# Layer 1's mixer: fewer, wider small products, B and C convolved as one block, and the slice bias as a float32r product

## The chip, the core and the metric

One Trainium2 chip, one of its cores. The metric is the device time in microseconds (us) of one execution of the whole program, as the median of several executions. A profiled execution gives the trace from which durations are read; it has a time of its own.

## The reference

Two layers on x (32 samples of 512 tokens by 256 features) with an integer adjacency matrix for each sample. Each layer is a graph stage and a feed-forward stage, each behind a layer norm and added to x. The change touches the second layer's feed-forward stage alone:

```python
fx = (x @ W_fx.T + b_fx).reshape(B, N, H, P).transpose(0, 2, 1, 3)
xm = (x @ W_x.T + b_x).reshape(B, N, H, P).transpose(0, 2, 1, 3)
sw = softmax((xm @ W_slice.T + b_slice) / temp, axis=-1)        # 8 heads, 64 slices
snorm = sw.sum(2)
st = einsum('bhnc,bhng->bhgc', fx, sw) / (snorm + 1e-05)[..., None]
ot = _hydra(st.transpose(0, 2, 1, 3).reshape(B, G, 512), ...)   # 64 slice tokens of 512
out = einsum('bhgc,bhng->bhnc', ot (by heads), sw)
return out.transpose(0, 2, 1, 3).reshape(B, N, 512) @ out_w.T + out_b

def _hydra(u, ...):                                  # a scan in both directions over 64 tokens
    zxbcdt = u @ in_w.T                              # z 512, x 512, B 64, C 64, dt 2 * 8
    dt = softplus(dt + dt_bias)                      # the second eight with the tokens reversed
    x, B, C = silu(causal convolution of width 3 over x, B and C)
    h = h * exp(-dt * exp(A_log)) + dt * B * x;  y = h . C        # each token, each head
    y = y_forward + y_backward + x * (x @ fcD.T + D)
    yg = y * silu(z)
    return (yg * rsqrt(mean(yg ** 2) + 1e-05) * norm_w) @ out_w.T
```

## The kernel before

Layer 0 takes the first 2400 us or so; near its end layer 1's constants are loaded and transposed a piece at a time between its steps (`load_T`). Layer 1 then goes through the samples with two generators. `attentions` prepares and computes the graph stage sample by sample. `mixer(g)` is the feed-forward stage of a pair of samples, g = 0 to 15. The mixer is the driver: each of its `yield n` gives credit by which the attention of later samples is advanced, so that both are woven into one program. From that the framework fixes the order of instructions on each engine, by its own estimate of when operands are ready; on the chip each engine goes through its list in order and waits on semaphores. PSUM banks of the mixer and most of the attention come from one pool ("any", four banks); work tiles of 128x512 of the mixer come from one rotating tag ("inner", six).

A round of the mixer, for samples 2g and 2g+1, in the order of the program:

- `slices` for each sample: layer norm (L1131, L1133), transposes (x4T, L1142); then for each of four token tiles the slice logits `lgp` (L1335, two float32 products of 512 columns), exp on ScalarE into `sw` (L1336), and on VectorE the product with `ebsl`, the exponential of the slice bias spread over all partitions (L1337), the sum over 64 slices of each head (L1340), its reciprocal (L1341) and the product with it (L1342). Then `yTp` (L1347) sums the tokens by slice weight, `swp` (L1352) transposes sw, and its copy on ScalarE gives the slice sums `rn` (L1353), of which VectorE takes the reciprocal (L1355).
- `tokens`: `uTp` (L1366) applies W_fx for each head. `rnp` (L1372) spreads the reciprocals over the partitions of their head: 16 products of 64x64, the weights being one column of rn repeated. `scale` (L1375) copies that out of PSUM, and VectorE makes `uT` (L1379, L1381): channels on partitions, 2 x 64 tokens in columns.
- `scan`, projection: `xp` (L1400, 16 products with 128 columns) gives x, `bcp` (L1409) B and C on 64 partitions each, in two column blocks; `dtp` (L1428) the step sizes in 16 products of 64x8 (forward and reversed halves put where they are needed) and 4 more of 128x16 (L1393); `zp` (L1393) z in 4 products of 512 columns. ScalarE copies x and B, C into padded tiles (`xpad` L1404, `bpad` L1413); VectorE convolves (`conv`, L1417 and L1419); ScalarE applies silu (L1455 for x, L1462 for B and C, L1450 for z) and, for the softplus, exp (L1437) and Ln (L1443), each change of function with a table load.
- `scan`, the rest: `gp` (L1487) is C times B, `segp` (L1491) the sums of log decays, from `seg` (L1481); `xtp`, `qp` (L1496, L1501); VectorE builds `mix` (L1505 to L1510); `yp` (L1517) is 16 products of 64x64, sample by sample, head by head; y (L1520 to L1522) is transposed (`yTp`, L1527), multiplied by the output weights (`oTp`, L1535); four products `msp` (L1543) put the mean squares on the partitions where `rms` (L1546, a power on GpSimd at L1547) is needed; `vp` (L1557) applies out_w, 64x64 weights and 256 columns, alternating between the two halves of the array.
- `unslice` for each sample: `outp` (L1567) and the sum into x (L1569), then the store.

In the attention, `att` (L1213) makes the weights on VectorE from `own`, a row that goes through DRAM and comes back spread over the partitions (L1200); `avp` and `adp` (L1249, L1254) multiply; `norm` (L1290 to L1304) is its layer norm on VectorE, with a power on GpSimd (L1300) in its middle; GpSimd also adds beta, the attention's bias and outb (L1167, L1189, L1328) and gathers x rows (L1154).

On PE a float32 product shows as two rows in the trace, each of which streams all columns; L434's product in layer 0, with both operands float32r, shows as one.

Of the kernel before, what the change touches and what calls it, by code (L numbers as in the profile page):

```python
# [8 lines left out]
F32 = mybir.dt.float32  # L9
# [855 lines left out]
def layer1_plain(tc, ident, eps, x2s, ranks, adj, w, out, over, ps):  # L865
# [35 lines left out]
    with ExitStack() as ctx:  # L901
# [14 lines left out]
        ones = ctile("ones", [P, P])  # L916
# [36 lines left out]
        bc_w = const("bc_w", [S, 2, KW], w["hy_conv_w"][DI:].rearrange("(c p) k -> p c k", p=S))  # L953
        bc_b = const("bc_b", [S, 2], w["hy_conv_b"][DI:].rearrange("(c p) -> p c", p=S))
        skip = const("skip", [P, H], w["hy_D"].partition_broadcast(P))
        dtb = ctile("dtb", [P, 4, H])
        for i in range(4):
            nc.sync.dma_start(dtb[:, i, :], w["hy_dt_bias"].partition_broadcast(P))
# [21 lines left out]

        wfxT = ctile("wfxT", [P, DC, DI])
        wsl = ctile("wsl", [P, DC, H, G])
        ebsl = ctile("ebsl", [P, H * G])
# [6 lines left out]
        with tc.tile_pool(name="raw", bufs=2, side="right") as raw:  # L990
# [16 lines left out]
            yield from load_T(inT, w["hy_in_w"], "in")  # L1007
# [48 lines left out]
            nc.sync.dma_start(ebsl, bsl_row.partition_broadcast(P))  # L1056
# [7 lines left out]
            nc.vector.tensor_reduce(most[:, 1:2], ebsl, AX.X, ALU.max)  # L1064
            nc.vector.tensor_reduce(most[:, 2:3], ebsl, AX.X, ALU.min)
            for i, limit, op in ((0, SMALL_S, ALU.is_gt), (1, SMALL_B, ALU.is_gt), (2, -SMALL_B, ALU.is_lt)):
                nc.vector.tensor_scalar(over[:, 2 * AH + i : 2 * AH + i + 1], most[:, i : i + 1], limit, None, op)
            nc.scalar.activation(ebsl, ebsl, AF.Exp)
# [249 lines left out]
        def slices(b, j, yT, rn):  # L1318
# [13 lines left out]
            for t in range(NT):  # L1332
                pf = psum("any", f"lgp{b}_{t}")
                for c in range(DC):
                    nc.tensor.matmul(pf, xnT[:, c, t * P : (t + 1) * P], wsl[:, c, :], start=c == 0, stop=c == DC - 1)  # L1335
                nc.scalar.activation(sw[:, t, :], pf, AF.Exp)  # L1336
                nc.vector.tensor_mul(sw[:, t, :], sw[:, t, :], ebsl)  # L1337
# [45 lines left out]
        def scan(g, uT):  # L1383
# [14 lines left out]
            for k in range(KC):  # L1398
                for c in range(KC):
                    nc.tensor.matmul(px[:, k * T : (k + 1) * T], inT[:, c, DI + k * P : DI + (k + 1) * P],  # L1400
                                     uT[:, c, :], start=c == 0, stop=c == KC - 1)
# [838 lines left out]
```

## Time and profile before

| What | us |
|---|---|
| median of 3 runs | 4462.75 (4462.54 to 4462.93) |
| profiled execution, its own time | 4459.08 |
| its span, first to last instruction | 4456.4 |
| PE busy | 3922.0 (88%) |
| VectorE (DVE) busy | 3347.2 (75%) |
| ScalarE (ACT) busy | 2291.6 (51%) |
| GpSimd (POOL) busy | 1718.8 (39%) |

Mean granted TensorE clock: 0.948. The rounds of the mixer can be told by `xp`, which starts at 2534.0, 2661.9, 2784.6 and so on to 4164.1, 4284.7 and 4390.4 us: 14 rounds of 125 us on average, and a last one with no attention beside it. In the tables of the profile, a group's line has engine, operation, output and inputs, shape, count; behind the first bar the busy time in us and the mean duration of one in ns; behind the second the engine's idle time just before these instructions and what ended it. A mean duration on PE holds the pipeline's depth, so the rate of products is read from the distance of their starts. The chain of work that ended last is followed back from the last instruction, at each step to what released it.

### The profile page before, as it was taken

The numbers are of one execution on the slowest core, as the hardware profiler recorded it, in microseconds if no ns is written. First come the engines' busy times: TensorE is split into PE (matmuls) and PEld (weight loads), VectorE is DVE, ScalarE is ACT, GpSimd is POOL, SyncE is SP. The second block draws the span as 40 slices with busy tenths as digits, with TensorE's granted clock in tenths as the row PEclk, the third lists the DMA queues.
The fourth block names the chain that finished last, engine by engine and source line by source line (L and its number), as shares of the span: only waits on it lengthen the run. The fifth ranks groups of instructions, "written<-read, shape, count | busy, mean of one in ns | idle before, by whom it ended". The sixth has DMA issues, their size and how long they took to land.

```text
span 4456.4 us, 57911 instructions
## 1 busy us (share of the span) xinstructions
PE 3922.0 (88%) x20311; PEld 2470.6 (55%) x20311; DVE 3347.2 (75%) x7008; ACT 2291.6 (51%) x4756; POOL 1718.8 (39%) x2036
## 2 busy tenths in 40 slices
PE   5568898899988999888997899999999999999987
PEld 4454565566656656545554455555555555555555
DVE  6668887897788987877766777767677877778763
ACT  3345565566564665556654544544545444454433
POOL 2357644664446644454314232332222232332220
PEclk8679999999999999989998999999999999999998
DMA  5546543664436543564422111111111111111100
GB/s 133 160 144 223 190 130 122 210 200 139 156 117 213 187 147 129 162 201 167 138 81 67 36 53 57 56 48 58 51 43 42 53 55 55 58 48 58 41 15 16
DMA packets 235107, 474.21 MB, mean 106 GB/s; under 512 B 38299, under 2 KB 114075, under 8 KB 234804
## 3 DMA queue, kind: packets, MB, share of 16 engines
q0 software_dynamic: 98688, 315.94, 22.2%
q1 hardware_dynamic: 136116, 154.46, 11.0%
q8 instruction: 162, 2.65, 0.2%
q14 instruction: 141, 1.16, 0.1%
HBM read 413.16 MB, written 57.16 MB: 106 GB/s over the span
## 4 chain that ended last, share of the span: by engine, by line
DVE 34%; PE 32%; DMA 11%; issue 9%; POOL 9%; ACT 5%; SPq 0%; POOLq 0%; DVEq 0%; ACTq 0%
DVE att L1213 5%; DVE acc L637 4%; PE clsp L623 3%; PE avp L1249 3%; PE po L652 3%; PE gatep L623 3%; DMA rows<-table,xs 2%; PE yTp L1347 2%; DVE sw L1337 2%; DVE sw L1342 2%; DVE best L598 2%; DMA rows<-table,tops 2%; DVE sst L1340 2%; DMA best<-table,xs 2%; PE xp L1400 1%
## 5 line engine op out<-in xcount | busy, mean ns | idle before, releaser
L623 PE MATMUL clsp<-xnT,wc 128*128 128x512 f32 x1024 | 520.8, 627 | 49.7 <-ACT cls L625 37.6
L623 PE MATMUL gatep<-xnT,wg 128*128 128x512 f32 x1024 | 499.8, 607 | 10.5 <-ACT gate L625 7.7
L652 PE MATMUL po<-wd,acc 128*128 128x256 f32 x2048 | 455.4, 381 | 6.1 <-DVE acc L641 3.8
L1213 DVE SCALAR_TENSOR_TENSOR att<-own,other,mask 128x512 f32<-128x512 f32 x512 | 392.9, 796 | 79.0 <-DMA own<-ownd 79.0
L652 PEld LDWEIGHTS po<-wd,acc 128*128 128x128 f32 x2048 | 388.3, 191 | 72.1 <-issue 9.2
L598 DVE SCALAR_TENSOR_TENSOR best<-rows,xs,best 128x1024 f32<-128x1024 f32 x212 | 274.4, 1295 | 121.9 <-ACT best L592 76.4
L637 DVE SCALAR_TENSOR_TENSOR acc<-past,fld,acc 128x512 f32<-128x512 f32 x448 | 345.7, 775 | 24.9 <-ACT past L636 16.9
L632 ACT ACTIVATE acc<-tz,fld 128x512 f32<-128x512 f32 x256 | 198.8, 777 | 269.3 <-PE tz L630 240.1
L623 PEld LDWEIGHTS gatep<-xnT,wg 128*128 128x128 f32 x1024 | 196.0, 196 | 252.3 <-issue 197.9
L636 ACT ACTIVATE past<-tz,fld 128x512 f32<-128x512 f32 x448 | 291.4, 693 | 68.1 <-DVE acc L637 66.6
L1347 PE MATMUL yTp<-sw,x 128*128 128x512 f32 x512 | 264.6, 655 | 64.3 <-DVE sw L1342 59.6
L595 POOL DMA_INDIRECT rows<-table,xs x212 | 249.5, 1177 | 171.6 <-DVE best L598 119.0
L1249 PE MATMUL avp<-att,hv 128*32 128x512 f32 x2048 | 298.9, 607 | 5.6 <-DVE att L1213 5.6
L623 PEld LDWEIGHTS clsp<-xnT,wc 128*128 128x128 f32 x1024 | 181.5, 198 | 188.1 <-issue 111.8
L434 PE MATMUL pm<-h,adj 128*128 128x258 f32 (+1 forms) x1024 | 181.2, 324 | 99.9 <-DVE keep L427 33.7
L1300 POOL TENSOR_TENSOR mu<-mu,eps 128x16 f32<-128x16 f32 x32 | 111.6, 3487 | 391.1 <-DVE mu L1299 391.0
L1335 PE MATMUL lgp<-wsl,x4T 128*128 128x512 f32 x512 | 242.8, 613 | 15.7 <-ACT sw L1336 6.8
L1154 POOL DMA_INDIRECT x<-x2s,ranks x128 | 135.9, 1062 | 298.1 <-DVE att L1213 148.1
L625 ACT ACTIVATE gate<-gatep,fld 128x512 f32<-128x512 f32 x256 | 175.5, 685 | 142.6 <-PE gatep L623 123.8
L553 POOL DMA_INDIRECT xs<-rows_of,order x128 | 156.1, 1219 | 221.5 <-DVE acc L637 100.8
L1567 PE MATMUL outp<-v,swT 128*128 128x256 f32 x1024 | 227.6, 381 | 0.0
L625 ACT ACTIVATE cls<-clsp,fld 128x512 f32<-128x512 f32 x256 | 176.1, 688 | 93.9 <-PE clsp L623 55.6
(599 smaller groups left out, 8978.1 us busy)
## 6 DMA issues: line engine op xcount, KB each, us to landing
adj<-in_adj POOLq DMA_DIRECT2D x128, 256.0 KB
ai<-in_adj SPq DMA_DIRECT2D x128, 256.0 KB
own<-ownd SPq DMA_DIRECT2D x128, 256.0 KB
rows_of<-keep SPq DMA_DIRECT2D x32, 550.0 KB
x<-in_x SPq DMA_DIRECT2D x32, 512.0 KB
x2s<-xs SPq DMA_DIRECT2D x32, 512.0 KB
out<-x SPq DMA_DIRECT2D x32, 512.0 KB
rows<-table,xs POOLq DMA_INDIRECT x212
```

The costliest lines, as they stand in the source:

```text
L595: nc.gpsimd.indirect_dma_start(out=row, out_offset=None, in_=table, in_offset=bass.IndirectOffsetOnAxis(ap=idxs[:, k : k + 1].bitcast(U32) ...
L598: nc.vector.scalar_tensor_tensor(m, row, vals[:, k : k + 1], m, ALU.add, ALU.max)
L623: nc.tensor.matmul(pf, wf[:, c, f * P : (f + 1) * P], xnT[:, c, :], start=c == 0, stop=c == DC - 1)
L625: nc.scalar.activation(o, pf, fn, bias=fld[:, f, bf : bf + 1], scale=1.0 if fn == AF.Gelu else 0.5)
L636: nc.scalar.activation(r, z, AF.Relu, bias=fld[:, f, AT + b : AT + b + 1])
L637: nc.vector.scalar_tensor_tensor(y, r, fld[:, f, CH + b : CH + b + 1], y, ALU.mult, ALU.add)
L652: nc.tensor.matmul(po[:, i, :], acc[f][:, t * P : (t + 1) * P], wd[:, f, :], start=f == 0, stop=f == FC - 1)
L1213: nc.vector.scalar_tensor_tensor(e, own[h], other[:, j, h : h + 1], mask[:, j, :], ALU.max, ALU.mult)
L1249: nc.tensor.matmul(pv[p][k * HW : (k + 1) * HW, :], hv[:, j, h, e : e + HW], weighed[b, h, j], **ends)
L1335: nc.tensor.matmul(pf, xnT[:, c, t * P : (t + 1) * P], wsl[:, c, :], start=c == 0, stop=c == DC - 1)
L1347: nc.tensor.matmul(py, xn[:, t, c * P : (c + 1) * P], sw[:, t, :], start=t == 0, stop=t == NT - 1)
L1567: nc.tensor.matmul(po[:, :D], swT[:, k, t * P : (t + 1) * P], v[:, k, :], start=k == 0, stop=k == KC - 1)
```

## The change

- Slice bias: the logits' bank starts with a product of two partitions by 512 columns, both operands float32r (a row of ones as weights, `brow` as the moving operand: the bias rounded to float32r and, on the second partition, what the rounding left), and the product with `ebsl` on VectorE is gone. `ebsl` is not made; `brow` is.
- Slice norms: VectorE makes `spread`, the reciprocals times an identity, 128x512, and one product with `same` (ones in the two diagonal blocks of 64) takes the place of the 16 of `rnp`.
- Projection: the columns of `inT` are put in the order dt, z, x, B, C. B and C come from one set of 4 products with 128 outputs, on 128 partitions; dt and the first half of z from 4 products of 272 columns into the same bank, the second half of z from 4 of 256. The reversed halves of dt are put in place by four small VectorE sums instead of products. `bc_w`, `bc_b`, `bpad` and `bcT` are 128 partitions high, and B and C's convolution is written ahead of x's.
- `gp` and `yp` loop over samples inside and heads (or directions) outside.
- `msp` is gone: four small VectorE operations write `rms` across partitions.

The diff, without the constants' shapes:

```diff
+        same = ctile("same", [P, P])
+        nc.gpsimd.memset(same, 0.0)
+        ident2 = ctile("ident2", [P, C])
+        for i in range(P // C):
+            half = slice(i * C, (i + 1) * C)
+            nc.gpsimd.memset(same[half, half], 1.0)
+            nc.gpsimd.tensor_copy(ident2[half], ident[half, half])
...
-        ebsl = ctile("ebsl", [P, H * G])
+        brow = cst.tile([2, H * G], F32R, tag="brow", name="brow")
...
-            yield from load_T(inT, w["hy_in_w"], "in")
+            yield from load_T(inT[:, :, 2 * H :], w["hy_in_w"][:DT0], "in")
+            yield from load_T(inT[:, :, : 2 * H], w["hy_in_w"][DT0:], "dt")
...
-            nc.sync.dma_start(ebsl, bsl_row.partition_broadcast(P))
+            both, least = (raw.tile([P, DI], F32, tag=f"raw{DI}", name=f"bias{i}")[:2] for i in range(2))
+            nc.sync.dma_start(both, bsl_row.partition_broadcast(2))
+            nc.scalar.copy(brow, both)
+            nc.vector.tensor_sub(least, both, brow.bitcast(F32))
+            nc.vector.tensor_scalar(least, least, ident[:2, 1:2], None, ALU.mult)
+            nc.vector.scalar_tensor_tensor(brow, brow.bitcast(F32), ident[:2, 0:1], least, ALU.mult, ALU.add)
...
-            nc.scalar.activation(ebsl, ebsl, AF.Exp)
...
                 pf = psum("any", f"lgp{b}_{t}")
+                nc.tensor.matmul(pf, short_ones[:2], brow, start=True, stop=False)
                 for c in range(DC):
-                    nc.tensor.matmul(pf, xnT[:, c, t * P : (t + 1) * P], wsl[:, c, :], start=c == 0, stop=c == DC - 1)
+                    nc.tensor.matmul(pf, xnT[:, c, t * P : (t + 1) * P], wsl[:, c, :], start=False, stop=c == DC - 1)
                 nc.scalar.activation(sw[:, t, :], pf, AF.Exp)
-                nc.vector.tensor_mul(sw[:, t, :], sw[:, t, :], ebsl)
                 s = sw[:, t, :].rearrange("p (h g) -> p h g", h=H)
...
         def tokens(g, yT, rn, uT):
+            spread = inner(f"spread{g}").rearrange("p (k j g) -> p k j g", k=KC, j=GB)
+            four = [P, KC, GB, G]
+            nc.vector.tensor_tensor(spread, rn.rearrange("p j k -> p k j").unsqueeze(3).to_broadcast(four),
+                                    ident2.unsqueeze(1).unsqueeze(1).to_broadcast(four), ALU.mult)
 
             pu, pn = psum("any", f"uTp{g}"), psum("any", f"rnp{g}")
-            uv, nv = (p.rearrange("p (k j g) -> p k j g", k=KC, j=GB) for p in (pu, pn))
+            uv = pu.rearrange("p (k j g) -> p k j g", k=KC, j=GB)
             for k in range(KC):
                 for i in range(P // C):
                     half, h = slice(i * C, (i + 1) * C), k * (P // C) + i
                     for c in range(DC):
                         nc.tensor.matmul(uv[half, k], wfxT[:, c, h * C : (h + 1) * C], yT[:, c, h],
                                          start=c == 0, stop=c == DC - 1)
-            for k in range(KC):
-                for i in range(P // C):
-                    half = slice(i * C, (i + 1) * C)
-                    for j in range(GB):
-                        nc.tensor.matmul(nv[half, k, j, :], rn[:, j, k : k + 1].to_broadcast([P, C]), ident[:, half],
-                                         start=True, stop=True)
+            nc.tensor.matmul(pn, same, spread.rearrange("p k j g -> p (k j g)"), start=True, stop=True)
             scale = inner(f"scale{g}")
...
                 for c in range(KC):
-                    nc.tensor.matmul(px[:, k * T : (k + 1) * T], inT[:, c, DI + k * P : DI + (k + 1) * P],
-                                     uT[:, c, :], start=c == 0, stop=c == KC - 1)
+                    x0 = 2 * H + DI + k * P
+                    nc.tensor.matmul(px[:, k * T : (k + 1) * T], inT[:, c, x0 : x0 + P], uT[:, c, :],
+                                     start=c == 0, stop=c == KC - 1)
             xpad = sb.tile([P, KC, GB, LP], F32, tag="xpad", name=f"xpad{g}", bufs=1)
             nc.gpsimd.memset(xpad[:, :, :, : KW - 1], 0.0)
             nc.scalar.copy(xpad[:, :, :, KW - 1 :], px.rearrange("p (k j l) -> p k j l", k=KC, j=GB))
-            pb = psum("any", f"bcp{g}")
-            for i in range(2):
-                c0 = 2 * DI + i * S
-                for c in range(KC):
-                    nc.tensor.matmul(pb[:S, i * T : (i + 1) * T], inT[:, c, c0 : c0 + S], uT[:, c, :],
-                                     start=c == 0, stop=c == KC - 1)
-            bpad = sb.tile([S, 2, GB, LP], F32, tag="bpad", name=f"bpad{g}", bufs=1)
-            nc.gpsimd.memset(bpad[:, :, :, : KW - 1], 0.0)
-            nc.scalar.copy(bpad[:, :, :, KW - 1 :],
-                           pb[:S, : 2 * T].rearrange("p (k j l) -> p k j l", k=2, j=GB))
+            pb, pz = psum("any", f"bcp{g}"), psum("any", f"zp{g}")
+            for c in range(KC):
+                nc.tensor.matmul(pb[:, :T], inT[:, c, DIN - P :], uT[:, c, :], start=c == 0, stop=c == KC - 1)
+            first = 2 * H + DI // 2
+            tok_matmul(pb[:, T : T + first], 0, first)
+            tok_matmul(pz[:, : DI // 2], first, DI // 2)
+            bpad = sb.tile([P, GB, LP], F32, tag="bpad", name=f"bpad{g}", bufs=1)
+            nc.gpsimd.memset(bpad[:, :, : KW - 1], 0.0)
+            nc.scalar.copy(bpad[:, :, KW - 1 :], pb[:, :T].rearrange("p (j l) -> p j l", j=GB))
...
 
-            pd = psum("any", f"dtp{g}")
-            for j in range(GB):
-                for i in range(2):
-                    for c in range(KC):
-                        nc.tensor.matmul(pd[i * G : (i + 1) * G, j * H : (j + 1) * H],
-                                         uT[:, c, j * G : (j + 1) * G],
-                                         inT[:, c, DT0 + i * H : DT0 + (i + 1) * H],
-                                         start=c == 0, stop=c == KC - 1)
-            tok_matmul(pd[:, 2 * H : 4 * H], DT0, 2 * H)
+            pd = pb[:, T : T + 2 * H]
             sp = sb.tile([P, 5, 4 * H], F32, tag="sp", name=f"sp{g}")
             v, e, u, r, dt = (sp[:, i, :] for i in range(5))
-            nc.vector.tensor_add(v, pd[:, : 4 * H], dtb.rearrange("p i h -> p (i h)"))
+            nc.vector.tensor_add(v[:, 2 * H :], pd, dtb.rearrange("p i h -> p (i h)"))
+            for i in range(2):
+                for j in range(GB):
+                    half = slice(j * G, (j + 1) * G)
+                    nc.vector.tensor_add(v[i * G : (i + 1) * G, j * H : (j + 1) * H],
+                                         pd[half, i * H : (i + 1) * H], dtb[half, 0, :])
             nc.vector.scalar_tensor_tensor(e, v, -1.0, v, ALU.mult, ALU.min)
...
 
-            pz = psum("any", f"zp{g}")
-            tok_matmul(pz, 0, DI)
             z = sb.tile([P, DI], F32, tag="z", name=f"z{g}", bufs=1)
-            nc.scalar.activation(z, pz, AF.Silu)
+            nc.scalar.activation(z[:, : DI // 2], pb[:, T + 2 * H : T + first], AF.Silu)
+            nc.scalar.activation(z[:, DI // 2 :], pz[:, : DI // 2], AF.Silu)
+            bcT = sb.tile([P, GB, G], F32, tag="bcT", name=f"bcT{g}", bufs=1)
+            cpad = sb.tile([S, GB, G + 2], F32, tag="cpad", name=f"cpad{g}", bufs=1)
+            nc.gpsimd.memset(cpad[:, :, 0 : G + 2 : G + 1], 0.0)
+            conv(bpad, bc_w, bcT)
+            for half, dst in ((slice(0, S), bcT[:S]), (slice(S, P), cpad[:, :, 1 : G + 1])):
+                nc.scalar.activation(dst, bcT[half], AF.Silu, bias=bc_b[half])
             xT = inner(f"xT{g}")
             for k in range(KC):
                 dst = chunks(xT)[:, k, :]
                 conv(xpad[:, k], conv_w[:, k, :], dst.rearrange("p (j l) -> p j l", j=GB))
                 nc.scalar.activation(dst, dst, AF.Silu, bias=conv_b[:, k : k + 1])
-            bcT = sb.tile([S, 2, GB, G], F32, tag="bcT", name=f"bcT{g}", bufs=1)
-            cpad = sb.tile([S, GB, G + 2], F32, tag="cpad", name=f"cpad{g}", bufs=1)
-            nc.gpsimd.memset(cpad[:, :, 0 : G + 2 : G + 1], 0.0)
-            for i in range(2):
-                conv(bpad[:, i], bc_w[:, i, :], bcT[:, i])
-                dst = bcT[:, 0] if i == 0 else cpad[:, :, 1 : G + 1]
-                nc.scalar.activation(dst, bcT[:, i], AF.Silu, bias=bc_b[:, i : i + 1])
-
-
...
             pg = psum("any", f"gp{g}")
-            for j in range(GB):
-                for i in range(2):
-                    nc.tensor.matmul(pg[j * G : (j + 1) * G, i * G : (i + 1) * G], bcT[:, 0, j, :],
+            for i in range(2):
+                for j in range(GB):
+                    nc.tensor.matmul(pg[j * G : (j + 1) * G, i * G : (i + 1) * G], bcT[:S, j, :],
                                      cpad[:, j, 2 * i : 2 * i + G], start=True, stop=True)
...
             py = psum("any", f"yp{g}")
-            for j in range(GB):
-                half = slice(j * G, (j + 1) * G)
-                for h in range(H):
+            for h in range(H):
+                for j in range(GB):
+                    half = slice(j * G, (j + 1) * G)
                     nc.tensor.matmul(py[half, h * C : (h + 1) * C], heads(mix)[half, h, :],
...
 
-            pm = psum("any", f"msp{g}")
+            rms = sb.tile([P, GB], F32, tag="rms", name=f"rms{g}")
             for j in range(GB):
                 for i in range(P // C):
-                    nc.tensor.matmul(pm[i * G : (i + 1) * G, j : j + 1], ident[:, j * G : (j + 1) * G], ms,
-                                     start=True, stop=True)
-            rms = sb.tile([P, GB], F32, tag="rms", name=f"rms{g}")
-            nc.vector.tensor_scalar(rms, pm[:, :GB], 1.0 / DI, LN_EPS, ALU.mult, ALU.add)
+                    nc.vector.tensor_scalar(rms[i * G : (i + 1) * G, j : j + 1], ms[j * G : (j + 1) * G], 1.0 / DI, LN_EPS,
+                                            ALU.mult, ALU.add)
             nc.gpsimd.tensor_tensor(rms, rms, eps[:, 1:2].to_broadcast([P, GB]), ALU.pow)
```

More of the change, by code (lines that the diff above doesn't have):

```diff
@@ L914, in psum @@
             return ps.tile([P, N], F32, tag=tag, name=name)
-        ones = ctile("ones", [P, P])
+        short_ones = cst.tile([P, P], F32R, tag="ones", name="ones")
+        ones = short_ones.bitcast(F32)
         nc.gpsimd.memset(ones, 1.0)
@@ L952, in layer1_plain @@
         conv_b = const("conv_b", [P, KC], w["hy_conv_b"][:DI].rearrange("(c p) -> p c", p=P))
-        bc_w = const("bc_w", [S, 2, KW], w["hy_conv_w"][DI:].rearrange("(c p) k -> p c k", p=S))
-        bc_b = const("bc_b", [S, 2], w["hy_conv_b"][DI:].rearrange("(c p) -> p c", p=S))
+        bc_w = const("bc_w", [P, KW], w["hy_conv_w"][DI:])
+        bc_b = const("bc_b", [P, 1], w["hy_conv_b"][DI:].rearrange("(p o) -> p o", o=1))
         skip = const("skip", [P, H], w["hy_D"].partition_broadcast(P))
-        dtb = ctile("dtb", [P, 4, H])
-        for i in range(4):
+        dtb = ctile("dtb", [P, 2, H])
+        for i in range(2):
             nc.sync.dma_start(dtb[:, i, :], w["hy_dt_bias"].partition_broadcast(P))
@@ L1063, in layer1_plain @@
             nc.vector.tensor_reduce(most[:, 0:1], pn, AX.X, ALU.max)
[L1064 to L1065 removed]
+            nc.gpsimd.memset(most[:, 1:], 0.0)
+            nc.vector.tensor_reduce(most[:2, 1:2], both, AX.X, ALU.max)
+            nc.vector.tensor_reduce(most[:2, 2:3], both, AX.X, ALU.min)
             for i, limit, op in ((0, SMALL_S, ALU.is_gt), (1, SMALL_B, ALU.is_gt), (2, -SMALL_B, ALU.is_lt)):
                 nc.vector.tensor_scalar(over[:, 2 * AH + i : 2 * AH + i + 1], most[:, i : i + 1], limit, None, op)
[L1068 removed]
         se = ctx.enter_context(tc.tile_pool(name="e1", bufs=2, side="right", reuse_waits="tile"))
@@ L1484, in scan @@
             pg = psum("any", f"gp{g}")
-            for j in range(GB):
-                for i in range(2):
-                    nc.tensor.matmul(pg[j * G : (j + 1) * G, i * G : (i + 1) * G], bcT[:, 0, j, :],
+            for i in range(2):
+                for j in range(GB):
+                    nc.tensor.matmul(pg[j * G : (j + 1) * G, i * G : (i + 1) * G], bcT[:S, j, :],
                                      cpad[:, j, 2 * i : 2 * i + G], start=True, stop=True)
```

## The prediction

> **What bounds the kernel now.** I read the busy times of stretches first, then the chain that ended last, then the groups by line, then one group's timeline. Layer 1 (from 2410 us) is sixteen rounds of the mixer, two samples each. The first stretches below are one round, cut at the mixer's own stages.
>
> ```profile
> core 0: us, PE busy (x) PEld busy (x) DVE busy (x) ACT busy (x) POOL busy (x), PEclk, DMA share, GB/s
> 3664.00:3672.70 8.70, 8.70 (x92) 8.08 (x92) 6.38 (x17) 3.52 (x5) 3.34 (x1) 1.00 0.06 23
> 3672.70:3690.30 17.60, 17.60 (x149) 8.25 (x147) 14.19 (x41) 14.89 (x32) 1.57 (x6) 1.00 0.07 16
> ...
> 3700.00:3782.00 82.00, 73.98 (x375) 41.75 (x377) 62.73 (x121) 33.98 (x92) 26.36 (x20) 0.98 0.20 65
> ```
>
> From the projection (xp, 3664) to the end of yp PE never stops; in the 82 us after it, where both samples' softmax lies, PE is idle 8 us. Who ends that idle time stands in the groups and in the timeline:
>
> ```profile
> L1347 PE MATMUL yTp<-sw,x 128*128 128x512 f32 x512 | 264.6, 655 | 64.3 <-DVE sw L1342 59.6 <-DVE sst L1341 2.7 <-ACT ai L1094 0.6
> L1335 PE MATMUL lgp<-wsl,x4T 128*128 128x512 f32 x512 | 242.8, 613 | 15.7 <-ACT sw L1336 6.8 <-DVE x L1569 5.5 <-ACT x4T L1143 1.9
> L1337 DVE TENSOR_TENSOR sw<-sw,ebsl 128x512 f32<-128x512 f32 x128 | 106.1, 834 | 10.2 <-ACT sw L1336 10.2
> L1340 DVE TENSOR_REDUCE sst<-sw 128x8 f32<-128x512 f32 x128 | 86.6, 681 | 0.9
> ```
>
> ```profile
> 3731.76 3.27 DVE L1337 TENSOR_TENSOR sw<-sw,ebsl 128x512 f32<-128x512 f32 x1
> 3732.09 2.38 POOL L1167 TENSOR_TENSOR x<-x,beta 128x1024 f32<-128x1024 f32 x1
> 3742.65 3.70 PE L1347 MATMUL yTp<-sw,x 128*128 128x512 f32 x8 [1.62 <-DVE sw L1342]
> 3774.05 5.96 PE L1347 MATMUL yTp<-sw,x 128*128 128x512 f32 x10 [2.98 <-DVE sw L1342]
> ```
>
> yTp waits for the last normalized tile: 60 us in all. The chain says the same; its pieces (start, length) in one round:
>
> ```profile
> 3664.02 3.77 PE xp L1400 x32
> 3667.79 1.89 PE bcp L1409 x16
> 3669.68 1.20 PE dtp L1428 x32
> 3670.88 0.99 PE dtp L1393 x8
> 3671.87 3.53 PE zp L1393 x8
> ...
> 3682.00 0.39 PE gp L1487 x8
> ...
> 3689.11 1.89 PE yp L1517 x32
> ...
> 3699.25 0.33 PE msp L1543 x8
> ...
> 3731.84 3.19 DVE sw L1337
> ```
>
> So a round has two halves: from xp to minep PE's order is the path; from there to the next xp it is DVE's (with POOL and two DMAs), PE beside it nearly as long. A float32 product is two rows of the trace.
>
> **The change part by part**, per round of 125 us (3664 to 3789), all prices start to start.
>
> *Softmax, L1337.* Eight DVE products go. One takes 0.60 us where DVE runs without a pause (the chain's other sw pieces, and sst beside them), so 8 x 0.60 = 4.8 us, all in the half that DVE sets. The mean of 834 ns holds some stretched ones like the 3.27 us above, beside a POOL product; I take no gain for these, since the next DVE product may meet the same POOL row.
>
> By the Trainium skill, "SBUF — State Buffer", section "SBUF: two separate sides", a DVE product with two SBUF inputs and a POOL operation lock one another out, and elsewhere on the page a reduce never does. The rows agree as far as they go: sst L1340 has a mean of 681 ns and no long ones. By the rule the 128 x (834 - 683) = 19 us above L1337's median would go too, and the time would be 19 us under my sum; by the row of att, which meets POOL as well, they pass to it.
>
> *Bias product.* PE gets eight, each one row of 512 columns. No row has this shape. Nearest is L434, whose h and adj are float32r too: seven of 256 columns span 1.08 us, the last one's 0.37 us of pipeline included, so (1.08 - 0.37)/6 = 0.118 us, and 0.24 us for 512. The upper end is that of a float32 product, 2 x 0.43 = 0.86 us (lgp). I take 0.24: 8 x 0.24 = 1.9 us. Cover: PE's waits in front of yTp, 1.62 + 2.98 us here. Price on the path 0; without cover +1.9, at the upper end 6.9 - 4.6 = +2.3.
>
> *Slice norms (tokens).* rnp's 32 rows (1.4 us) become two of 0.43. DVE gets the product that makes spread, 0.60 us, between the reciprocal and rnp. In the changed program's order more moves: DVE does L1298 and L1301 (1.13 each) ahead of uT instead of behind it, and PE a turn of attention (avp x16 rows, adp: 1.9 us) ahead of rnp instead of ahead of yp. Laid along the order from the end of swp: rn at 1.3, L1294 2.4, L1355 and att 3.15, spread 3.75, rnp 4.7, scale 5.3; L1298 and L1301 to 6.0, uT's four 7.15, mask 7.75, last uT 8.35. Before, 6.3 (3781.76 to 3788.08). So +2.1 us.
>
> *Projection.* B and C as one product of 128 outputs: 8 rows x 0.118 instead of 16. dt and z: 8 rows of 272 columns (0.23) and 8 of 256 (0.216, outp's rate) instead of 32 + 8 + 8 rows. 1.89 + 1.20 + 0.99 + 3.53 = 7.61 becomes 0.94 + 1.86 + 1.73 = 4.53: -3.1 us on PE, and one bank fewer. But what is late next is gp, which needs the silu of C. ScalarE's order does not put B and C first: all four x silus, both z halves and an adjacency row come before the exp of dt. From the end of uT: POOL's power on mu 3.5, DVE L1303 4.75, att, L1304, att 7.2, x convolutions 12 x 0.28 to 10.5, last x silu 11.2, z 12.0, L1093 12.8, table load and exp 14.3, load and B 15.9, load and Ln 17.45, load (1.28 each) and C 19.1. Before: 17.1, and gp at 18.2. PE, with 3.1 us less to do and a turn moved away, is there at about 14.7 and waits 4.4 us. So gp is 1.0 later; yp, which waits for mix, comes at 26.2 instead of 27.0 because the moved turn no longer stands before it: -0.85. Of the 3.1 us, then, nearly nothing arrives. If ScalarE kept up, gp could come 3.5 us earlier.
>
> *yp and gp by alternating halves.* yp's 32 rows take 1.83 to 1.89 us, 58 ns each, eight products in one quarter of the array after another. vp, which alternates halves, does 64x256 in 106 ns a row where outp's 256 columns take 216: two at a time. So 29 ns if nothing else limits, 37 by dtp's smallest rows: 0.93 to 1.2, -0.9 or -0.65; I take -0.9, since y L1521 waits for it. gp: 0.1, nothing.
>
> *rms.* msp's 0.33 us goes from PE's path: -0.33. Four small DVE rows (0.1 to 0.17 each) replace one; DVE waits there for msp now (21 us in all). The four small sums for dt on 64 partitions likewise add 0.4 us in front of the exp, counted in the 14.3.
>
> *Once.* The 256 KB broadcast and an exp go; three DVE rows of 0.6, a ScalarE copy and a few POOL rows come, beside layer 0's end: 0.
>
> Sum of a round: -4.8 + 2.1 - 0.85 - 0.9 - 0.33 = -4.8 us. Fifteen rounds: -72. The last round has no attention to hide in: the bias products follow one another with no wait before yTp (+1.9), spread +0.6 less 0.3, the projection hides behind the same ScalarE chain (PE waits 4.36 us before gp there), yp's 3.29 at a low clock halves (-1.6): +0.6. Together -71: 4459.1 (span 4456.4 and 2.7 around it) becomes 4388; the median of the runs is 3.7 above the profiled one, so 4392.
>
> The waits also cost clock: in the trace's clock records the grant falls to 0.5 for 3.41 us at 3773.5, at the end of the 2.98 us gap. That goes with the gap, but the new gap before gp can bring it back; I net this to zero. The Trainium skill, "TensorE: Matmul & The Clock Gate", section "What's actually happening", speaks against the change: an idle window of about 3.4 us throttles. Here 2.98 us was enough, and by the rule a gap of 4.4 us each round costs 1.7 us more, 26 us in all.
>
> **Rivals.**
> 1. *Everything adds.* C's silu comes no later than PE does, the half-clock stretches go, and PE sets the round: PE's work -3.1 - 0.5 - 0.9 - 0.33 + 1.9 = -2.9, its waits before yTp (4.6) with them: -7.5 x 15 = -113, 4350. For: PE is busy 115.5 of 125 us. Against: ScalarE's order above.
> 2. *Eaten.* The 4.8 us of DVE arrive only at the one yTp that waits 2.98: -3.0 + 2.1 - 0.9 = -1.8 x 15 = -27, 4436. For: DVE waits for POOL (hv L1202) and for own's DMA between the samples. The bias product at float32's price gives nearly the same: 4392 + 2.3 x 15 = 4427.
> 3. *Slower: the wait before gp.* If DVE's saving is lost in its waits for POOL and DMA, and uT's 2.1 and gp's 1.0 stay, with 1.7 for a stretch at half clock (3.41 us at 0.5, as at 3773.5) and the -0.9 of yp kept, a round grows by 3.9: +58, 4520. It decides from the point where DVE's 4.8 shrinks below 0. For: in the view of waits DVE stands 100.2 us in 18 samples for hv L1202, 5.6 us each. Against: the sw chain lies behind that wait, not before it.
> 4. *No change*: the two halves only trade places, 4463.
>
> **How the numbers follow.** Forecast 0.53 (its own range 4360 to 4425), everything adds 0.21, eaten 0.13, slower 0.10, no change 0.03. 4345 to 4445 leaves out the slower case, the no-change case and the ends of the first: about 2 in 10. Changes within 0.2% (9 us) can't be told from none: faster 0.87, same 0.03, slower 0.10.
>
> **What would show it.** Right: yTp's idle time falls from 64 to under 20 us with DVE's sw named seldom; lgp's new row starts 0.24 us before its neighbour; gp's idle time (4.4 us now) grows to over 40 us, released by ScalarE's cpad; yp's 32 rows take about 1 us. Wrong: gp without a wait (then rival 1), yTp still waiting about 2 us each (then 2), a round over 125 us with PE at half clock behind gp (then 3).

## The result, and the profile after

The changed kernel takes 4530.15 us (median of 4, 4523.96 to 4536.33) where the kernel before takes 4462.84: a ratio of 1.0147, 95% interval 1.013 to 1.0165. The forecast was 4392, the other sign.

The stretches of one round of the changed kernel, cut at the same stages as before (projection; from there to the end of yp; a half-clock stretch within it; the two softmaxes with attention):

```profile
core 0: us, PE busy (x) PEld busy (x) DVE busy (x) ACT busy (x) POOL busy (x), PEclk, DMA share, GB/s
3719.70:3727.80 8.10, 8.10 (x57) 7.52 (x57) 5.97 (x13) 2.17 (x3) 2.87 (x1) 1.00 0.01 2
3727.80:3750.60 22.80, 15.14 (x126) 7.85 (x124) 14.56 (x43) 17.75 (x38) 4.25 (x6) 0.88 0.10 24
3738.35:3741.76 3.41, 3.41 (x19) 1.69 (x13) 0.29 (x1) 3.36 (x6) 0.10 (x1) 0.50 0.02 5
3760.00:3837.30 77.30, 75.75 (x377) 41.97 (x376) 55.74 (x111) 33.77 (x90) 26.18 (x19) 1.00 0.23 69
```

In the softmax half PE is now busy 75.8 of 77.3 us, and DVE, which the prediction took to set it, is busy 55.7. The middle stretch, where PE never paused before, takes 22.8 us of which PE works 15.1, and its mean clock is 0.88. The groups by line (busy, mean ns, then idle time and its releasers):

```profile
L1352 PE MATMUL lgp<-wsl,x4T 128*128 128x512 f32 x512 | 253.1, 618 | 0.6 <-ACT x4T L1159 0.6
L1363 PE MATMUL yTp<-sw,x 128*128 128x512 f32 x512 | 248.2, 623 | 30.9 <-DVE sw L1358 29.3
...
L1350 PE MATMUL lgp<-brow,ones 2*128 2x512 f32 x128 | 62.3, 491 | 3.5 <-DVE x L1575 2.1 <-ACT sw L1353 1.0
...
L1525 PE MATMUL yp<-xk,mix 64*64 64x64 f32 x512 | 23.1, 254 | 25.9 <-DVE mix L1518 25.9
...
L1495 PE MATMUL gp<-cpad,bcT 64*64 64x64 f32 x128 | 8.9, 272 | 58.1 <-ACT cpad L1467 58.1
```

yTp's idle time fell from 64 to 31 us, but gp now has 58 and yp 26. TensorE's timeline around them (start, length, and in brackets the wait):

```profile
3732.28 1.44 PE L1270 MATMUL adp<-att,hv 128*32 128x512 f32 x6
3738.10 0.50 PE L1495 MATMUL gp<-cpad,bcT 64*64 64x64 f32 x8 [4.37 <-ACT cpad L1467]
3738.53 1.97 PE L1499 MATMUL segp<-seg,seg_l 128*64 128x512 f32 x4
...
3744.10 1.48 PE L1196 MATMUL hp<-wa,x3T 128*128 128x264 f32 x4
3748.68 1.97 PE L1525 MATMUL yp<-xk,mix 64*64 64x64 f32 x32 [3.11 <-DVE mix L1518]
```

segp takes 1.97 us, at half clock, where the kernel before has

```profile
3682.31 1.08 PE L1491 MATMUL segp<-seg,seg_l 128*64 128x512 f32 x4
```

The last product for mix, on VectorE, ends at the moment yp starts, and takes 2.72 us where its neighbours take 0.69:

```profile
3745.19 0.69 DVE L1517 TENSOR_TENSOR mix<-mix,back 128x512 f32<-128x512 f32 x1
3745.91 2.72 DVE L1518 TENSOR_TENSOR mix<-mix,decay 128x512 f32<-128x512 f32 x1
```

GpSimd's timeline has this beside it, of the same length:

```profile
3745.39 2.70 POOL L1344 TENSOR_TENSOR x<-x,outb 128x1024 f32<-128x1024 f32 x1 [6.57 <-ACT x L1149]
```

In the kernel before, the same sum started behind that product, after yp (3689.09):

```profile
3688.34 0.69 DVE L1510 TENSOR_TENSOR mix<-mix,decay 128x512 f32<-128x512 f32 x1
3690.28 2.37 POOL L1328 TENSOR_TENSOR x<-x,outb 128x1024 f32<-128x1024 f32 x1 [6.52 <-ACT x L1133]
```

ScalarE's timeline ahead of gp shows what PE waits for: one table load of 1.28 us per small function, with C's silu last.

```profile
3731.55 1.28 ACT L1449 ACT_TABLE_LOAD   x1
3732.85 0.23 ACT L1449 ACTIVATE sp<-sp 128x32 f32<-128x32 f32 x1
3733.10 1.28 ACT L1467 ACT_TABLE_LOAD   x1
3734.39 0.40 ACT L1467 ACTIVATE bcT<-bcT,bc_b 64x128 f32<-64x128 f32 x1
3734.81 1.28 ACT L1455 ACT_TABLE_LOAD   x1
3736.10 0.23 ACT L1455 ACTIVATE sp<-sp 128x32 f32<-128x32 f32 x1
3736.35 1.28 ACT L1467 ACT_TABLE_LOAD   x1
3737.65 0.40 ACT L1467 ACTIVATE cpad<-bcT,bc_b 64x128 f32<-64x128 f32 x1
```

A mean over rounds 2 to 14 of each trace, from one uTp to the next, is the measure for the rest of this text. "Waits" sums PE's gaps of over 60 ns, "clock" is half the time at a granted clock of 0.5, "work" is what remains:

| kernel | round us | waits | clock | work | median us (before beside it) |
|---|---|---|---|---|---|
| before | 124.8 | 8.6 | 2.5 | 113.7 | 4462.8 |
| changed | 128.5 | 11.2 | 4.6 | 112.7 | 4530.2 (4462.8) |
| e1 bias alone | 124.9 | 5.8 | 1.7 | 117.4 | 4462.0 (4459.8) |
| e2 projection alone | 129.0 | 12.3 | 5.9 | 110.8 | 4509.8 (4459.8) |
| e3 yp, small sums alone | 124.0 | 9.3 | 2.1 | 112.6 | 4448.6 (4459.8) |
| e4 changed, no spread | 127.3 | 10.1 | 4.3 | 112.9 | 4494.3 (4459.8) |
| e5 bias twice | 126.8 | 5.5 | 2.4 | 118.9 | 4493.2 (4457.8), one run |
| e6 bias in bfloat16 | 124.1 | 6.3 | 1.2 | 116.7 | 4454.1 (4457.8) |
| e7 projection, B and C ahead | 125.2 | 11.2 | 2.6 | 111.4 | 4457.6 (4457.8) |
| e8 order mended | 121.3 | 9.4 | 2.2 | 109.7 | 4406.2 (4457.8) |
| e9 changed again | 128.6 | 11.2 | 4.7 | 112.7 | 4523.8 (4459.8) |
| e10 changed, order mended | 124.7 | 8.5 | 2.4 | 113.8 | 4449.9 (4459.8) |
| e11 e8 with spread | 123.6 | 11.4 | 2.4 | 109.8 | 4440.5 (4459.8) |
| e12 e8 with bfloat16 bias | 122.2 | 7.6 | 0.8 | 113.9 | 4415.7 (4459.8) |
| e13 projection, POOL sum moved | 124.9 | 10.6 | 3.3 | 111.0 | 4458.5 (4455.9) |
| e14 changed, POOL sum moved | 126.9 | 10.3 | 3.8 | 112.7 | 4495.6 (4455.9) |

By stretches, the same means for the kernel before and the changed one, beside what the parts of the forecast come to there (e14 is the changed kernel with one GpSimd instruction moved, told below):

| stretch of a round | before | changed | difference | forecast | e14 |
|---|---|---|---|---|---|
| uTp to xp | 8.6 | 11.4 | +2.8 | +2.1 | 11.4 |
| xp to gp | 17.5 | 18.6 | +1.1 | +1.0 | 18.6 |
| gp to yp | 8.4 | 9.7 | +1.3 | -1.85 | 8.6 |
| yp to oTp | 5.5 | 5.55 | 0.0 | -0.9 | 5.0 |
| oTp to the next uTp (softmax) | 84.7 | 83.2 | -1.6 | -5.1 | 83.2 |

From the first xp to the last, the changed trace is 51 us longer (54 in e9, the same program). Of the 72 us between the two profiled spans, 22 more lie before the first xp, and the last round is a little shorter. Layer 1's first product stands at 2404.5 us instead of 2384.9; in e9 it stands at 2387.0, and in e2 and e13, whose programs differ from each other only in layer 1's mixer, at 2404.9 and 2390.5. So one and the same program can start layer 1 some 15 us earlier or later. e9's profiled execution is the shortest of its four, though: whether the change makes a late start more frequent, single traces can't tell. The rounds, 51 to 54 us, are the part of the 64 to 67 that is shown.

### The profile page after: what moved, and what is told of

Read it like the earlier page. It is cut to its first block, busy times and chain, and to the rows that moved or that the text cites. A ratio compares the mean times of both kernels' runs of the same rounds, so it can differ in the third digit from the quotient of the medians.

```text
span 4528.8 us, 55719 instructions
## 1 busy us (share of the span) xinstructions
PE 3943.9 (87%) x19191; PEld 2464.4 (54%) x19191; DVE 3307.5 (73%) x6963; ACT 2298.5 (51%) x4770; POOL 1714.1 (38%) x2042
## 3 DMA queue, kind: packets, MB, share of 16 engines
q1 hardware_dynamic: 135688, 154.19, 11.2%
## 4 chain that ended last, share of the span: by engine, by line
DVE 34%; PE 31%; DMA 10%; issue 9%; POOL 8%; ACT 7%; SPq 0%; another core or an unknown queue 0%; DVEq 0%; POOLq 0%; ACTq 0%
DVE att L1229 5%; DVE acc L637 4%; PE clsp L623 3%; PE lgp L1352 3%; PE gatep L623 3%; PE po L652 3%; PE yTp L1363 2%; DVE best L598 2%; PE hp L1196 2%; DMA rows<-table,xs 2%; DMA rows<-table,tops 2%; POOL mu L1316 1%; PE oTp L1543 1%; DVE acc L639 1%; PE avp L1265 1%
## 5 line engine op out<-in xcount | busy, mean ns | idle before, releaser
L1363 PE MATMUL yTp<-sw,x 128*128 128x512 f32 x512 | 248.2, 623 | 30.9 <-DVE sw L1358 29.3
L1352 PE MATMUL lgp<-wsl,x4T 128*128 128x512 f32 x512 | 253.1, 618 | 0.6 <-ACT x4T L1159 0.6
L434 PEld LDWEIGHTS pm<-h,adj 128*128 128x128 f32 x1024 | 153.1, 215 | 131.5 <-issue 72.7
```

The costliest lines, as they stand in the source:

```text
L434: nc.tensor.matmul(pm[:, : c1 - c0], a[:, i, t * P : (t + 1) * P], h[:, i, c0:c1], start=i + c0 == 0, stop=i + 1 == NT and c0 > 0)
L1363: nc.tensor.matmul(py, xn[:, t, c * P : (c + 1) * P], sw[:, t, :], start=t == 0, stop=t == NT - 1)
```

## The experiments

**The parts alone.** Each is the kernel before with some lines of the diff and no others.

e1: the bias product with its constant, in place of the DVE product.

```diff
+                nc.tensor.matmul(pf, short_ones[:2], brow, start=True, stop=False)
-                nc.vector.tensor_mul(sw[:, t, :], sw[:, t, :], ebsl)
```

> Before, with the bias product alone (eight float32r products of two rows per round instead of eight DVE products). Theory A (the product costs PE 0.62 us a tile, 5.0 us a round, so most of DVE's saving is lost): between 1 and 2 us off a round of 125, 4435 to 4450. My prediction's step (-4.8 a round, 1.9 hidden): 4385 to 4400. Theory D (the first layer is 20 us later because its transfers are delayed by what the change does to memory): first x3T0p near 2404 instead of 2385, and the time 20 above what the rounds give.

Measured: 1.0003 (0.9986 to 1.002), no change. Theory A was too kind: PE's work grows by 3.7 us a round (8 x 0.62 would be 5.0; where the rest goes was not traced), its waits and half clock shrink by 3.6. The groups:

```profile
L1354 PE MATMUL yTp<-sw,x 128*128 128x512 f32 x512 | 248.2, 624 | 28.0 <-DVE sw L1349 26.5
...
L1341 PE MATMUL lgp<-brow,ones 2*128 2x512 f32 x128 | 63.8, 502 | 7.2 <-DVE x L1576 6.8 <-ACT sw L1344 0.2
```

yTp's wait is more than halved, as meant, and 128 products stand in its place. Layer 1 began at 2389.7 us, so nothing here speaks for theory D.

e2: the projection (B and C as one product, dt and z as two, the old rest).

```diff
+            for c in range(KC):
+                nc.tensor.matmul(pb[:, :T], inT[:, c, DIN - P :], uT[:, c, :], start=c == 0, stop=c == KC - 1)
+            tok_matmul(pb[:, T : T + first], 0, first)
+            tok_matmul(pz[:, : DI // 2], first, DI // 2)
```

> Before, with the projection alone (B and C as one product of 128 outputs, dt and z as two products, silus and convolutions in the new program order). Theory A (PE comes to gp early and waits there for ScalarE's silu of C, then runs at half clock): xp to yp grows by 2 to 3 us a round, time 4490 to 4510. My prediction's step (gp +1.0, yp's turn moved away): between 4450 and 4480. Rival (the projection is harmless and the loss lies in the spread product): at most 4463, xp to yp shorter than 25.9 us.

Measured: 1.01 (1.0072 to 1.0129), +50 us. xp to gp grew by only 0.7 us a round; gp to yp grew by 2.1, and yp to oTp by 2.1 too, where no product was added. The timeline and a stretch of it:

```profile
3729.92 1.47 PE L1181 MATMUL hp<-wa,x3T 128*128 128x264 f32 x4
3734.51 3.31 PE L1511 MATMUL yp<-xk,mix 64*64 64x64 f32 x32 [3.12 <-DVE mix L1504]
3737.75 5.64 PE L1181 MATMUL hp<-wa,x3T 128*128 128x264 f32 x12
```

```profile
3733.01:3743.25 10.24, 8.74 (x45) 7.28 (x46) 2.83 (x3) 2.89 (x14) 0.90 (x1) 0.50 0.19 51
```

Within the 3.1 us without a product the clock falls to 0.50, where it stays for 10.24 us, and hp's twelve rows take 5.64 us where they take 2.94 elsewhere. Over the round, PE does 2.9 us less and loses 3.6 to waits and 3.4 to the clock. What theory A says of the cause is open until e13.

e3: yp's products by alternating halves, and the small sums without msp.

```diff
-            for j in range(GB):
-                half = slice(j * G, (j + 1) * G)
-                for h in range(H):
+            for h in range(H):
+                for j in range(GB):
+                    half = slice(j * G, (j + 1) * G)
```

> Before, with yp's products by alternating halves and the small sums without msp. By my prediction -0.9 and -0.33 a round: 4445. If yp's products do not overlap (the changed kernel's yp to oTp was no shorter than before's, 5.55 against 5.54): 4456 to 4463.

Measured: 0.9974 (0.9962 to 0.9987), -11 us, between the two. PE's work falls by 1.0 us a round, and 0.8 of it arrives.

e4: the changed kernel with the old rnp.

```diff
 against the changed kernel
-            nc.tensor.matmul(pn, same, spread.rearrange("p k j g -> p (k j g)"), start=True, stop=True)
+                        nc.tensor.matmul(nv[half, k, j, :], rn[:, j, k : k + 1].to_broadcast([P, C]), ident[:, half],
+                                         start=True, stop=True)
```

> The changed kernel with the old slice norms (32 small products, no spread on DVE). Theory A (uT to xp grew by 2.85 us a round through the spread product and what the order moves ahead of uT): 4530 - 15 x 2.85 = 4487, uTp to xp back at 8.6. Rival (it is not spread but the order that the shorter projection brings, which stays here): 4515 to 4535.

Measured: 1.0068 (1.0047 to 1.0089), 29.5 us below the changed kernel's run e9 by the medians; the rounds differ by 1.2, 18 us in fifteen. The time is near theory A's, but not its reason: uTp to xp was 10.5, not 8.6. e1, without spread, has 10.4 as well, so the order that comes with the bias product makes 1.8 of the 2.8 us by itself, and spread adds 0.9.

**The bias product's price.** e5 issues it twice, each with half the bias:

```diff
-                nc.tensor.matmul(pf, short_ones[:2], brow, start=True, stop=False)
+                for i in range(2):
+                    nc.tensor.matmul(pf, short_ones[:2], brow, start=i == 0, stop=False)
```

> The bias product alone, issued twice in a row for each tile with half the bias. If its price is the change of type (float32r between float32 products), the second starts 0.24 us after the first, the rate of the 256-column rows; if float32r with 2 partitions or 512 columns is slow by itself, 0.42 us. A round grows by 1.9 or by 3.4 us over the run with one.

The timeline of one tile:

```profile
3621.77 0.73 PE L1343 MATMUL lgp<-brow,ones 2*128 2x512 f32 x2
3622.43 1.98 PE L1345 MATMUL lgp<-wsl,x4T 128*128 128x512 f32 x4
```

Neither: the second starts 0.34 us after the first, and the float32 row 0.32 after the second (medians of the trace), between 0.24 and 0.42. The round grows by 1.9. So the product itself is 0.33. A single one takes 0.42 until the float32 row behind it starts, that row 0.53 instead of 0.43, and a float32 row ahead of it 0.52 instead of 0.43. About half of the 0.62 us is the change of type.

e6 has the bias as three bfloat16 rows:

```diff
-        brow = cst.tile([2, H * G], F32R, tag="brow", name="brow")
+        brow = cst.tile([3, H * G], BF16, tag="brow", name="brow")
```

> The bias product alone, in bfloat16: three rows (the bias split in three parts) instead of two in float32r. If 0.62 us a tile is the change of type, it costs about the same: 4455 to 4465. If it is float32r's own rate: 0.24 us and nothing around it, 3 us of a round less on PE, 4420 to 4440.

Measured: 0.9996 (0.9981 to 1.0011). It takes 0.31 instead of 0.42, with the same 0.1 on either side: 0.51 a tile, 4.1 us a round. Cheaper, and still worth nothing.

**The order.** e7 is e2 with two orders forced at compile time (behind(a, b) puts b behind a on its own engine, without a wait):

```diff
+                one, _ = conv(xpad[:, k], conv_w[:, k, :], dst.rearrange("p (j l) -> p j l", j=GB))
+                behind(bc_end, one)
+                behind(c_silu, nc.scalar.activation(dst, dst, AF.Silu, bias=conv_b[:, k : k + 1]))
+            behind(c_silu, nc.scalar.activation(z[:, : DI // 2], pb[:, T + 2 * H : T + first], AF.Silu),
+                   nc.scalar.activation(z[:, DI // 2 :], pz[:, : DI // 2], AF.Silu))
```

> The projection alone, with two orders forced: on DVE the convolution of B and C before those of x, on ScalarE the silu of B and C before those of x and z. Theory A (PE's new waits before gp and yp, 3.9 us with 4.2 us of half clock a round in the run of the projection alone, come from ScalarE's order with its table loads between): the waits go, a round falls from 129.0 to 121 to 125, time 4400 to 4460. Rival (the waits come from DVE, whatever ScalarE does): 4490 to 4510.

Measured: 1.0003 (0.9988 to 1.0018), 52 us below e2 with the same products. Its timeline has no wait before yp, and attention products between:

```profile
3688.66 0.45 PE L1489 MATMUL gp<-cpad,bcT 64*64 64x64 f32 x8 [1.42 <-ACT z L1465]
...
3697.11 1.06 PE L1255 MATMUL adp<-att,hv 128*32 128x512 f32 x6
3698.10 1.90 PE L1519 MATMUL yp<-xk,mix 64*64 64x64 f32 x32
```

The same products in another order lose nothing. Which part of the order did it, this run can't tell: mix's last product takes 0.69 us again too, and POOL's sum comes at 3700.86. The 2.3 us that PE is spared go into small waits (2.2 us between xp and gp). ScalarE has three table loads a round here, six in e2.

e8 goes further: B, C and dt are multiplied before x, the exp and log of dt come before every silu, with e3's edits; neither bias product nor spread.

```diff
+            for c in range(KC):
+                nc.tensor.matmul(pb[:, :T], inT[:, c, DIN - P :], uT[:, c, :], start=c == 0, stop=c == KC - 1)
+            tok_matmul(pb[:, T : T + first], 0, first)
...
+            nc.scalar.activation(e, e, AF.Exp)
+            for k in range(KC):
+                for c in range(KC):
+                    x0 = 2 * H + DI + k * P
...
+            ln = nc.scalar.activation(u, u, AF.Ln)
...
+                behind(ln, c_silu)
```

> The projection with B, C and dt computed before x, the exp and the log of dt before every silu (three table loads a round instead of six), and yp's and the small sums' new order; neither the bias product nor spread. Theory A: PE's work falls by 2.9 + 1.0 us a round without new waits: 121 a round, 4390 to 4410. Rival (PE's order behind uT is bound by DVE): 4445 to 4500.

Measured: 4406.2, ratio 0.988 (0.986 to 0.99): faster than both kernels. ScalarE:

```profile
3644.64 0.23 ACT L1430 ACTIVATE sp<-sp 128x32 f32<-128x32 f32 x1 [1.26 <-DVE sp L1429]
...
3647.30 1.28 ACT L1441 ACT_TABLE_LOAD   x1
3648.59 0.23 ACT L1441 ACTIVATE sp<-sp 128x32 f32<-128x32 f32 x1
3648.84 1.28 ACT L1453 ACT_TABLE_LOAD   x1
3650.13 0.40 ACT L1453 ACTIVATE bcT<-bcT,bc_b 64x128 f32<-64x128 f32 x1
3650.55 0.40 ACT L1453 ACTIVATE cpad<-bcT,bc_b 64x128 f32<-64x128 f32 x1
```

No load stands in front of this exp; B and C share one. In the rounds the log, the silus and decay's exp load once each: three loads of 1.28 us instead of six, as in e7. So the loads alone don't make the 51 us between e7 and e8: e3's edits, alone, are worth 11, and the rest comes with B, C and dt standing before x, which was not taken apart further.

**The changed kernel beside them.** e9 is the changed kernel again, without an edit.

> The changed kernel once more, beside the runs below, for their differences and for the first layer's time: 4520 to 4540 if the 20 us of the first layer belong to the change, 4505 to 4525 if they were the spread from run to run (the kernel before alone has shown 31 us of it).

Measured: 4523.8, ratio 1.0149 (1.0132 to 1.0166), as above. That lies in both ranges, so the median doesn't decide about layer 0.

e10 is the changed kernel with e8's order of the projection.

> The changed kernel whole, with only the order mended: B, C and dt before x on TensorE, B and C's convolution before x's on DVE, exp and log before every silu on ScalarE. Theory A (the order behind uT made most of the loss; bias 0, spread 1.2 us a round): 4415 to 4430. Rival (the parts are worth nothing together, PE and DVE both full in the softmax half): 4440 to 4470.

Measured: 0.9983 (0.9971 to 0.9994). The order is worth 74 us here (of all three engines together; they were not tried one by one), but the result is 44 above e8 and lies in the rival's range: my expectation was too low, since bias and spread each cost on this base. The next two show it, the bias in its cheaper form.

e11 adds spread to e8.

> The fastest so far (projection first, order forced, yp and small sums) with the spread product added. If spread costs what the changed kernel shows against the run without it (1.2 us a round): 4425. If only by the place where DVE's order puts it: 4406 or less, since PE has 1.0 us less to do.

Measured: 0.9965 (0.9954 to 0.9976), +34 us over e8, 2.2 us a round: more than either expectation. VectorE from the reciprocal of rn to the first rows of uT, in e11:

```profile
3640.53 0.16 DVE L1364 RECIPROCAL rn<-rn 128x4 f32<-128x4 f32 x1
...
3641.33 0.67 DVE L1370 TENSOR_TENSOR spread<-rn,ident 128x512 f32<-128x512 f32 x1
3641.94 1.21 DVE L1303 TENSOR_TENSOR av<-av,mu 128x1024 f32<-128x1024 f32 x1
...
3644.33 1.21 DVE L1307 TENSOR_REDUCE mu<-ht 128x16 f32<-128x1024 f32 x1
3645.46 1.11 DVE L1387 SCALAR_TENSOR_TENSOR uT<-uTp,bfx_eps,scale 128x128 f32<-128x128 f32 x4
```

and in e8:

```profile
3633.41 0.17 DVE L1356 RECIPROCAL rn<-rn 128x4 f32<-128x4 f32 x1
...
3635.96 1.13 DVE L1380 SCALAR_TENSOR_TENSOR uT<-uTp,bfx_eps,scale 128x128 f32<-128x128 f32 x4 [0.53 <-ACT scale L1376]
```

4.9 us instead of 2.6: spread itself and attention rows that the order puts in between. Which of the two weighs more was not tried.

e12 adds e6's bias product to e8.

> The fastest so far with the bias product in bfloat16. Bias and DVE product trade 4.8 us of DVE for 8 x 0.51 = 4.1 us of PE; alone that gave 0.7 us a round: 4395 to 4406. If PE is the bound in the softmax half now that the other half is shorter: above 4410.

Measured: 0.9904 (0.9887 to 0.992), 9.5 us above e8: PE's work grows by 4.1 us a round, its waits and half clock give back 3.2. The time is in the rival's range, but its reason isn't shown: oTp to uTp is 1.4 us shorter than in e8, and it is uTp to the projection that is 1.8 longer, as in e1.

**The collision.** e13 is e2, and e14 the changed kernel, with one GpSimd instruction moved: the sum of x and the output bias, in slices(), stands behind rms's power on GpSimd's own queue. The orders of TensorE, VectorE and ScalarE stay as they were. In e2 the two rows lie like this:

```profile
3731.73 2.72 DVE L1504 TENSOR_TENSOR mix<-mix,decay 128x512 f32<-128x512 f32 x1
3731.21 2.70 POOL L1329 TENSOR_TENSOR x<-x,outb 128x1024 f32<-128x1024 f32 x1 [6.11 <-ACT x L1134]
```

The edit:

```diff
+            add = nc.gpsimd.tensor_add(xt, xt, outb.unsqueeze(1).to_broadcast([P, NT, D]))
+            if pows:
+                tc.add_manual_dep(add.ins, pows[-1].ins.name,
+                                  mybir.DependencyInfo(mybir.DependencyClass.NoSync, mybir.DependencyReason.DATA),
+                                  reason="order")
...
+            pows.append(nc.gpsimd.tensor_tensor(rms, rms, eps[:, 1:2].to_broadcast([P, GB]), ALU.pow))
```

> The projection alone (e2), with one POOL product moved: the sum of x and the output bias is put behind rms's power on POOL, so that it no longer runs beside DVE's last product for mix; the orders of PE, DVE and ScalarE are the same as in e2. Theory C (in e2 that product of mix takes 2.1 us on average beside POOL's sum instead of 0.69, which makes PE's wait before yp 3.1 us instead of 1.1 and so brings the half clock): mix back at 0.69, no half clock behind yp, a round of 124 to 126, 4445 to 4475. Theory A alone (the missing attention turn makes the wait): mix may fall, but the half clock stays, 4485 to 4510.

> The changed kernel with the same one POOL sum moved and nothing else. Theory C: mix back from 1.6 us to 0.69, yp's wait falls below 1.2 us; the wait before gp (4.4 us in the round shown) and its half clock stay: 3 to 5 us a round less at most, 4455 to 4490. Theory A alone: 4505 to 4530.

Measured: e13 1.0007 (0.9986 to 1.0027), 51 us below e2 (47, each against the kernel before beside it); e14 1.0097 (1.0069 to 1.0126), 28 below e9 (24). Theory C holds in both, though in e14 the gain is less than it had: a round is 1.6 us shorter, and the time a little above its range. e13's timelines of VectorE, to be set beside the changed kernel's, and of TensorE, beside e2's:

```profile
3688.78 0.68 DVE L1509 TENSOR_TENSOR mix<-mix,back 128x512 f32<-128x512 f32 x1
3689.49 0.69 DVE L1510 TENSOR_TENSOR mix<-mix,decay 128x512 f32<-128x512 f32 x1
```

```profile
3690.24 1.90 PE L1517 MATMUL yp<-xk,mix 64*64 64x64 f32 x32 [1.08 <-DVE mix L1510]
3692.07 2.94 PE L1181 MATMUL hp<-wa,x3T 128*128 128x264 f32 x12
```

PE's wait is 1.08 us instead of 3.12, and yp and hp run at full clock (3.31 and 5.64 us in e2). In the whole trace, mix's last product is over 1.5 us long in 11 of 16 rounds of e2, 7 of the changed kernel, and in none of the kernel before, e7, e13 and e14. The 1.08 us that are left were not traced further. In e14 the wait before gp stays as it was, 3.3 us a round, and so does the half clock between gp and yp, 2.8 us a round (2.9 in the changed kernel).

## Why the prediction was wrong, point by point

The forecast's sum was -71 us. Of its signs, those of gp (58 us of idle time, released by cpad) and of yp's rows (1.15 us at full clock) came; yTp's idle time fell to 31 us and not under 20, and lgp's new row stands 0.42 us before its neighbour, not 0.24. In the same order of parts:

1. **Softmax and bias, -4.8 a round with the bias product at 0 (-72): failed, and it is the largest error.** Two steps. The price, "8 x 0.24 = 1.9 us", was taken from 256-column rows in an unbroken run of one type; it is 0.62 us a tile, 5.0 a round. And in the half "that DVE sets" PE waited only 4.6 us before yTp: removing DVE work can at most remove PE's waits there. e1 shows both: waits and half clock -3.6, work +3.7, sum 0. I had named the cover (4.6 us) but spent it once for the gain and once for the price.
2. **Projection, -0.85 and "I net this to zero" (-13): failed, +50 in e2.** That gp would wait for ScalarE's chain and come 1.0 later was right (+1.1). Two steps failed, and both show between gp and yp.
   - The clock, netted to zero. In the changed kernel PE waits 3.1 us a round before gp, and half clock between gp and yp costs 2.9 us a round, where the kernel before has none; over the whole round it costs 4.6 instead of 2.5. The sentence beside the zero, 1.7 us a round for a gap of 4.4, was near. This is the larger part of the changed kernel's loss here, and it stays in e14. Why PE waits longer before gp than in e2 (1.2) was not taken apart: e4 has 3.0, so it isn't spread. e10, with another order on three engines, has 1.0, and 1.2 of half clock.
   - "yp ... comes at 26.2 instead of 27.0" took mix's products at their length of before. In the new order ScalarE normalizes the next sample earlier against yp, GpSimd's sum for it starts earlier, and DVE's last product for mix meets it: 2.72 us for 0.69. In e2 that makes PE's wait before yp (2.1 us a round) and most of the half clock around it. e13 moves that one sum, and the 50 us of e2 are gone; in the changed kernel, where the two meet in 7 rounds of 16, it is worth 28 of the 64 us. The Trainium skill's rule, "SBUF — State Buffer", section "SBUF: two separate sides", of a two-input DVE product and a POOL operation shutting one another out agrees with these rows; I had weighed it for the removed L1337 alone, and not for the products that the change moves.
3. **Spread, +2.1 (+31): near in size, the cause only in part.** +29.5 by the medians of e9 and e4 (18 by their rounds) and +34 in e11, with rows that the order moves ahead of uT, as named. But in the changed kernel uTp to xp grew by 2.8 us, of which spread adds only 0.9: the bias product's order brings 1.8 without it (e1), which the sum didn't have.
4. **yp and msp, -0.9 and -0.33 (-18): right in kind, -11 in e3.** At full clock yp's 32 rows take 1.15 us in e3 against 1.90 before, -0.75 and not -0.9, and of 1.0 us less work 0.8 arrives. In the changed kernel half clock behind yp (0.8 us a round) eats it.

By the medians the parts are 2 + 50 - 11, and 30 for spread as taken out of the changed kernel: 71 us against 64 of the whole in e9. That they nearly add up is partly chance, since they overlap: the collision costs 50 us in e2 and 28 in the whole. Rival 3 came nearest with 4520, and largely by its mechanism: uT later, gp later, half clock behind gp. It did not have the collision, and it lost DVE's 4.8 us to DVE's own waits, where e1 shows PE's price for the bias product.

## What to carry to other kernels

When an engine on the path sheds work, give the saving no more than the waits of the engine beside it, and charge what is moved onto that engine against the same waits. When a change shifts one stage against the others, ask for every two-input VectorE product ahead of the bound engine which GpSimd row now falls beside it, and price the wait together with the slow clock behind it: here one unchanged GpSimd sum cost some 50 us in e2 and 28 in the changed kernel. Shorter products brought nothing here while a later result came through a chain of small steps (e2, e7, e13); with the products that feed that chain put first, the kernel gained 52 us (e8, with e3's 11 in it).

## What the hardware showed

- Between the first and the last xp of thirteen of these traces (e1 to e12 without e5, before and changed), gaps of PE of 2.6 us and more had a stretch at a granted clock of 0.5 starting in them or within 3.5 us behind in 98 of 124 cases (67 of 92 for those under 3.4 us); of the gaps between 0.9 and 1.7 us, 36 of 359 had one. The stretches last 3.41 us or a multiple, mostly 3.41 to 13.65. The Trainium skill, "TensorE: Matmul & The Clock Gate", section "What's actually happening", gives an idle window of about 3.4 us, free-running; gaps shorter than that were enough here.
- A product of 512 columns takes 0.33 us in float32r with 2 partitions, and 0.31 in bfloat16 with 3 up to the float32 row behind it; a change of type costs about 0.1 us on each of the float32 rows around it.
